# A GRU's recurrent products in two streams, one for each half of the batch

## The chip, the cores and the metric

The kernel runs on one core of a Trainium2 chip. The metric is the device time of one execution in microseconds; a time given as measured is the median of several runs.

## The reference

A GRU runs over 128 time steps for a batch of 64 with 512 features; the hidden size is 512. All is float32.

```
z = sigmoid([x_t, h] @ Wz + bz)
r = sigmoid([x_t, h] @ Wr + br)
h_cand = tanh([x_t, r * h] @ Wh + bh)
h_new = (1 - z) * h + z * h_cand
h_next = tanh(h_new @ Wp + bp)   where (t + 1) % 4 == 0 and t < 127, else h_new
out[t] = x_t + h_new
```

The step takes h_next to the next step. The parts with x_t do not depend on h and can be computed ahead; the parts with h can't.

## The kernel before

Two kinds of matmul share TensorE. The first are the recurrent gates R, Z and H (and P after every fourth step, the tanh above). A gate is `gate` (line 211): for each of four slices k of the hidden size, `products` (line 199) issues four matmuls, for two halves of the batch (h = 0, 1; 32 rows each) and two halves c of the columns. Each writes 32 PSUM partitions, a quarter, so the four stand side by side in the array; half 0 has the first 64 partitions and half 1 the last 64. One such group of four matmuls is called a unit here; a gate is four units of 256 columns. In the profile a float32 matmul is two instructions, so a unit is eight.

The second kind computes the x parts for later steps, by a scheme of products over blocks that needs fewer multiplications (`batch`, line 438), with sums prepared on GpSimd (POOL) and put together there. These are units of 192 columns, 14 to a batch. They stand in a list, and `fill(n)` (line 377) issues the next n of them. They write five scratch PSUM banks, q, r, a, x and y. At the end of certain units ScalarE (ACT) copies a bank to the tiles cx or cq and VectorE (DVE) adds banks into mb; a later unit that writes the bank again waits for that.

A step t issues on PE: gate R; gate Z; fill(places[0]); gate H; fill(places[1]); and if the step has one, gate P; fill(places[2]). The numbers are in PLACES (line 574), by the step's place in a period of eight (u), with HEAD and TAIL for the first and last steps. The order on every engine is the order in which the program issues the instructions; no scheduler changes it.

Behind gate R, for one half after the other, ACT takes the sigmoid (`crossed`, line 226, two instructions), DVE multiplies it with h (rh, line 672) and transposes the product (rhT, line 233): gate H needs it. Behind Z, ACT takes four sigmoids and DVE computes keep = (z - 1) * h (line 686). Behind H, for each half ACT takes the tanh (c), DVE multiplies it with z (line 716) and subtracts keep (line 725); then one transpose of both halves makes hT, which the next gate needs. `seed` (line 368) copies the x parts of the next step into a gate's PSUM tile on ACT as soon as the gate's old content has been read; the matmuls accumulate onto it.

PSUM tiles: rec_r holds R and P, rec_z holds Z and the z values, rec_h holds H and the r values (lines 152 to 160). Each is a bank; accesses of different engines to one bank wait for each other, also to different parts of it.

At the end of a step POOL does sums of the batches and adds h to the x tile, and SyncE (SP) issues the stores and the loads of later x.

Of the kernel before, what the change touches and what calls it, by code (L numbers as in the profile page):

```python
# [18 lines left out]
def kernel(  # L19
# [14 lines left out]
    nc = tc.nc  # L34
# [119 lines left out]
    rec = [ps_c.tile([P, S, 2, J], F32, name=f"rec_{n}") for n in "rzh"]  # L154
    P_ = 3
    r, z = rec[H_][:, 1], rec[Z][:, 1]

    def gate_ps(i):
        return rec[0][:, 1] if i == P_ else rec[i][:, 0]
# [4 lines left out]
    )  # L164

# [33 lines left out]
    def products(ps, lhs, rhs, start=False):  # L199
        for h in range(S):  # L200
            for c in range(2):
                nc.tensor.matmul(  # L202
                    ps[part(2 * h + c)],
                    lhsT=lhs(h),
                    rhs=rhs(c),
                    start=start,
                    stop=True,
                    skip_group_check=True,
                )

    def gate(i, lT, w):
        for k in range(K):
            products(
                gate_ps(i), lambda h: lT[:, h, ts(k, V)], lambda c: quarters(w)[:, c, k]
            )

    def product(ps, lT, w, k, start=False):
        c0, s0 = divmod(k, C)
        products(
            ps.rearrange("p (d j) -> p d j", d=2),  # L220
            lambda h: lT[:, c0, s0 * B + h * V : s0 * B + (h + 1) * V],
            lambda c: quarters(w)[:, c, k],
            start,
        )

    def crossed(dst, h, ps, func):
        for d in range(2):
            nc.scalar.activation(  # L228
                dst[ts(d, 2 * V), h, :], ps[ts(h, 2 * V), d, :], func
            )  # L230
# [137 lines left out]
    def seed(i, t):  # L368
        if t < T:
            nc.scalar.copy(  # L370
                gate_ps(i).rearrange("p d (c n) -> p d c n", c=C),
                G[t][:, :, :, i, :].rearrange("p c d n -> p d c n"),
            )

    queue = []

    def fill(n):
        for _ in range(min(n, len(queue))):
            unit, end = queue.pop(0)
            unit()  # L380
            if end is not None:
                end()
# [13 lines left out]

    def plain(t):
        g, i = divmod(t, Q4)
        order = [(e, k) for e in range(3) for k in range(K)]
        if t == Q4 - 1:  # L400
            order = [(e, k) for k in range(K) for e in range(3)]
        units = [
            lambda e=e, k=k: product(
                banks(t)[e], xT[g][:, i], wx[:, :, e, :], k, k == 0 and e != Z
            )
            for e, k in order
        ]
        return [(u, None) for u in units[:-1]] + [(units[-1], lambda: add_bias(t, (R, Z, H_)))]

    def plain_last():  # L410
        def units(t, gates, ks):
            return [
                lambda e=e, k=k: product(
                    banks(t)[e], xT[LAST][:, t % Q4], wx[:, :, e, :], k, k == 3 and e != Z
                )
                for k in ks
                for e in gates
            ]

        seq = [(u, None) for t in (T - 2, T - 1) for u in units(t, (R, Z, H_), (3,))]  # L420
        for t, gates in ((T - 2, (R, Z, H_)), (T - 1, (R, Z)), (T - 1, (H_,))):
            us = units(t, gates, (2, 0, 1))
            seq += [(u, None) for u in us[:-1]]
            seq.append((us[-1], lambda t=t, gates=gates: add_bias(t, gates)))
        return seq
# [12 lines left out]
    def batch(n, ms):  # L438
# [3 lines left out]
        def unit(ps, m, j, e, start):  # L442
            g, i = ms[m]
            a, b = terms(i)[e]
            left, right = lhs(g, a, j), factor(b, j)
            products(
                ps[:, m].rearrange("p d (g u) -> p d g u", g=3),
                lambda h: left[:, ts(h, V)],
                lambda c: right[:, c::2],
                start and m == 0 and e == 0,  # L450
            )

        def units(ps, j, start):
            return [
                lambda m=m, e=e: unit(ps, m, j, e, start)
# [15 lines left out]
        x_ps = x_two[len(T2) % 2]  # L471
# [26 lines left out]
        for ps, j, start, end in (  # L498
            (a_ps, 2, True, None),
            (x_ps, 7, True, end_x),  # L500
            (q_ps, 1, True, end_q),
            (r_ps, 5, True, end_r),
            (x_ps, 4, False, None),
            (q_ps, 6, False, end_q2),
            (r_ps, 3, False, end_r2),
        ):
            us = units(ps, j, start)
            seq += [(u, None) for u in us[:-1]] + [(us[-1], end)]
# [60 lines left out]
    def pair_right(a, p1, x_, g=1):  # L569
# [5 lines left out]
        (1, 8, 5), (1, 9, 0), (4, 8, 0), (6, 8, 0), (1, 8, 5), (6, 8, 0), (0, 8, 0), (1, 11, 0),  # L575
    )
    HEAD = {0: (12, 12, 0), 1: (8, 6, 0), 2: (16, 12, 0), 3: (8, 6, 8), 4: (6, 10, 0)}
# [10 lines left out]
    h = h_init  # L588
    hT = new_T("hT", "hT_init")
    both = [plain(0), plain(1)]  # L590
    for e in range(3):
        parts = [us[4 * e : 4 * e + 4] for us in both]

        queue.extend(sum(map(list, zip(*parts)), []) if e == R else sum(parts, []))
        fill(4)
        if e == H_:
            for i in range(3):
                seed(i, 0)
        fill(4)
        if e == R:  # L600
            spread(scratch[3], slice(0, 2), (R, H_))
            spread(scratch[1], slice(2, 3), (Z,))
            nc.gpsimd.tensor_sub(bias_d, bias_x[:, 1], bias0)
        if e == Z:
            for s_ in range(S):
                turn(hT[:, s_, :], h[:, s_, :])
# [3 lines left out]
    for t in range(T):  # L610
        g, j = divmod(t, Q4)
        prop = j == CHUNK - 1 and t < T - 1
        last = t == T - 1
        duo, u = divmod(t - 3, 8)
        even, odd = FIRST + 2 * duo, FIRST + 2 * duo + 1
        here = duo >= 0 and even * Q4 < T
        places = HEAD.get(t) or TAIL.get(t) or PLACES[u]
        if t == 0:
            queue.extend(plain(2) + plain(3))
        elif t == 1:  # L620
            queue.extend(batch((1, 0), [(1, 1), (1, 2)]))
        elif t == 2:
            queue.extend(batch((1, 1), [(1, 10), (1, 11)]) + batch((1, 2), [(1, 8), (1, 9)]))
        elif t == 3:
            queue.extend(batches(FIRST))
        elif u == 7:
            queue.extend(batches(even + 2))
        if t == T - 10:
            queue.extend(
# [5 lines left out]
        def join(n):  # L635
            if t == 0:
                join_x(0, 2 + n)
            elif t == 1:
                join_x(1, 2 + n)
            elif t == 2:  # L640
                join_x(2, n)
            elif t == 4:
                join_x(3, 2 * n)
                join_x(3, 2 * n + 1)
            elif duo >= 0 and u in (5, 6):
                join_x(even + 2, 2 * (u - 5) + n)
            elif duo >= 1 and u in (1, 3):
                join_x(odd, u - 1 + n)

        gate(R, hT, wh[R])  # L650
# [17 lines left out]
        rh = two.tile([P, S, J], F32, tag="rh", name=f"rh_{t}")  # L668
        rhT = new_T("rhT", f"rhT_{t}")
        for s_ in range(S):  # L670
            crossed(r, s_, gate_ps(R), AF.Sigmoid)
            nc.vector.tensor_mul(rh[:, s_, :], r[:, s_, :], h[:, s_, :])  # L672
            turn(rhT[:, s_, :], rh[:, s_, :])
        if t != 3:
            seed(R, t + 1)
        if prop:
            nc.scalar.copy(gate_ps(P_), bias_p)
        if last:
            seed(H_, t)
        join(0)  # L680

        gate(Z, hT, wh[Z])
        keep = two.tile([P, S, J], F32, tag="keep", name=f"keep_{t}")
        for s_ in range(S):
            crossed(z, s_, gate_ps(Z), AF.Sigmoid)
        nc.vector.scalar_tensor_tensor(  # L686
            out=keep, in0=z, scalar=1.0, in1=h, op0=ALU.subtract, op1=ALU.mult
        )
        join(1)
        if t == 1:  # L690
            sum_raw34(1)
        if t == 3:
            seed(R, t + 1)
        seed(Z, t + 1)
        if last:
            nc.gpsimd.tensor_sub(xr[g][:, j], xr[g][:, j], keep)
        if t == 0:
            sum_outer()
            for i in (6,):
                sum_inner(i, nc.gpsimd)  # L700
                sum_inner_1(i, nc.gpsimd)
        if t == 2:
            for n in range(2, 4):
                join_x(2, n)
        fill(places[0])
        if t == T - 7:
            reload()

        gate(H_, rhT, wh[H_])
        h_new = two.tile([P, S, J], F32, tag="h", name=f"h_{t}")  # L710
        hT = None if last else new_T("hT", f"hT_{t}")
        cand = two.tile([P, S, J], F32, tag="c", name=f"c_{t}")
        for s_ in range(S):
# [141 lines left out]
```

## Time and profile before

| | |
|---|---|
| measured, median of 3 runs | 1372.75 us (1371.66 to 1373.72) |
| profiled execution, its own time | 1372.32 us |
| its span | 1370.3 us |
| granted TensorE clock, mean over the span | 0.996 |
| busy share: PE, PEld, DVE, ACT, POOL | 96%, 68%, 55%, 53%, 65% |
| first Z gate starts at | 33.48 us |
| last Z gate starts at | 1359.68 us |

A line of the timeline reads: start in us, duration in us, engine, source line, operation, written tile <- read tiles, shape, xcount of merged instructions, and in brackets the engine's idle time before it and what ended it. PE is the matmul, PEld the weight load that goes with each. The ends of matmuls are modelled; their starts are measured.

### The profile page before, as it was taken

Reading aid. Unit: us, or ns where it says so; the run is one execution under the profiler, and the core shown is the slowest. Engines: PE = TensorE matmul, PEld = TensorE weight load, DVE = VectorE, ACT = ScalarE, POOL = GpSimd, SP = SyncE. Lnnn points to the kernel's source line nnn. Section 1 sums busy time; section 2 is a strip of 40 time slices with the busy share of each in tenths; the row PEclk is TensorE's granted clock in tenths of the full one; section 3 lists DMA queues with packets and bytes.
Section 4 is the critical chain, followed back from the end, with each engine's and each line's share of the span. In section 5 each row is a group of like instructions: output and inputs, shape, how many; then the busy total and the mean of one; then the engine's idle time right before and its main releaser. Section 6 shows DMA issues by size and latency. Waiting matters only on the chain. (4 is left out here: it accounts for less than half of the span.)

```text
span 1370.3 us, 60091 instructions
## 1 busy us (share of the span) xinstructions
PE 1315.0 (96%) x26024; PEld 925.3 (68%) x26024; DVE 753.5 (55%) x2036; ACT 730.2 (53%) x2401; POOL 887.3 (65%) x1030
## 2 busy tenths in 40 slices
PE   7999999999999999999999999999999999999986
PEld 3566767676676766767676676766767676676654
DVE  1645555555555555556555555555556555555533
ACT  1345555555555555555555555555555555555544
POOL 3577757777576766757777576776757767576420
PEclk9999999999999999999999999999999999999999
DMA  8401112101111111112101111111111101111030
GB/s 188 99 19 49 48 41 57 34 20 47 49 49 34 36 50 30 49 38 54 39 19 48 49 49 34 36 46 34 49 36 52 44 19 49 49 33 34 17 102 17
DMA packets 114705, 63.15 MB, mean 46 GB/s; under 512 B 13160, under 2 KB 109672, under 8 KB 114440
## 3 DMA queue, kind: packets, MB, share of 16 engines
q1 hardware_dynamic: 113412, 58.44, 17.0%
q8 instruction: 204, 3.34, 1.1%
q10 hardware_dynamic: 772, 0.72, 0.2%
q14 instruction: 61, 0.50, 0.1%
q0 software_dynamic: 256, 0.14, 0.1%
HBM read 42.47 MB, written 16.78 MB: 43 GB/s over the span
## 5 line engine op out<-in xcount | busy, mean ns | idle before, releaser
L228 ACT ACTIVATE rec_h<-rec_r 64x128 f32<-64x128 f32 x512 | 128.0, 250 | 344.2 <-PE rec_r L202 288.3
L202 PE MATMUL rec_h<-wh,rhT 128*32 128x256 f32 x4096 | 274.2, 381 | 4.3 <-DVE rh L672 3.7
L202 PEld LDWEIGHTS rec_h<-wh,rhT 128*32 128x32 f32 x4096 | 166.4, 110 | 75.0 <-DVE rh L672 24.7
L202 PE MATMUL rec_r<-wh,hT 128*32 128x256 f32 x3072 | 184.9, 381 | 14.4 <-DVE hT L233 13.3
L202 PE MATMUL rec_z<-wh,hT 128*32 128x256 f32 x3072 | 183.8, 379 | 0.0
L792 POOL TENSOR_TENSOR xr<-xr,h 128x256 f32<-128x256 f32 x127 | 93.1, 733 | 134.4 <-DVE h L725 123.0
L228 ACT ACTIVATE c<-rec_h 64x128 f32<-64x128 f32 x512 | 139.3, 272 | 68.0 <-PE rec_h L202 61.6
L526 POOL TENSOR_TENSOR cp<-mb,mb 128x768 f32<-128x768 f32 x75 | 137.1, 1828 | 43.5 <-DVE mb L495 39.9
L526 POOL TENSOR_TENSOR mb<-mb,mb 128x768 f32<-128x768 f32 x58 | 106.2, 1830 | 82.7 <-DVE mb L495 82.7
L202 PEld LDWEIGHTS rec_r<-wh,hT 128*32 128x32 f32 x3072 | 96.6, 110 | 87.2 <-DVE hT L233 27.2
L672 DVE TENSOR_TENSOR rh<-rec_h,h 128x128 f32<-128x128 f32 x192 | 55.9, 291 | 172.6 <-ACT rec_h L228 172.6
L202 PEld LDWEIGHTS rec_z<-wh,hT 128*32 128x32 f32 x3072 | 103.8, 110 | 61.9
L228 ACT ACTIVATE rec_z<-rec_z 64x128 f32<-64x128 f32 x512 | 128.0, 250 | 22.3 <-PE rec_z L202 7.2
L716 DVE TENSOR_TENSOR rec_z<-c,rec_z 128x128 f32<-128x128 f32 x256 | 75.7, 296 | 99.2 <-ACT c L228 82.5
L526 POOL TENSOR_TENSOR cp<-mb 128x768 f32<-128x768 f32 x47 | 86.2, 1835 | 60.7 <-DVE rec_z L716 59.2
L468 ACT COPY cq<-scratch_q 128x384 f32<-128x384 f32 (+1 forms) x214 | 102.3, 478 | 21.8 <-PE scratch_q L202 19.5
L531 POOL TENSOR_TENSOR mb<-mb,bias_x 128x768 f32<-128x768 f32 x35 | 64.2, 1833 | 45.5 <-DVE mb L495 45.5
L686 DVE SCALAR_TENSOR_TENSOR keep<-rec_z,h 128x256 f32<-128x256 f32 x96 | 40.8, 425 | 91.4 <-ACT rec_z L228 91.4
L491 DVE TENSOR_TENSOR mb<-scratch_q,cx 128x384 f32<-128x384 f32 (+1 forms) x107 | 58.1, 543 | 49.0 <-ACT cq L468 49.0
L233 DVE STREAM_TRANSPOSE rhT<-rh 128x128 f32<-128x128 f32 x256 | 79.8, 312 | 8.7
L725 DVE TENSOR_TENSOR h<-rec_z,keep 128x128 f32<-128x128 f32 x254 | 74.0, 292 | 16.4
L370 ACT COPY rec_z<-cp 128x256 f32<-128x256 f32 x128 | 48.2, 377 | 61.9 <-DVE keep L686 61.9
(157 smaller groups left out, 2805.6 us busy)
## 6 DMA issues: line engine op xcount, KB each, us to landing
out_dram<-xr SPq DMA_DIRECT2D x249, 64.0 KB, 1.8
xr<-in_x_dram SPq DMA_DIRECT2D x248, 64.0 KB, 2.2
xs<-in_x_dram SPq DMA_DIRECT2D x240, 64.0 KB, 2.2
wx<-in_L_cond_Wz_dram SPq DMA_DIRECT2D x4, 256.0 KB, 8.4
wx<-in_L_cond_Wh_dram SPq DMA_DIRECT2D x4, 256.0 KB, 10.3
wh<-in_L_cond_Wr_dram SPq DMA_DIRECT2D x4, 256.0 KB, 9.0
wh<-in_L_cond_Wz_dram SPq DMA_DIRECT2D x4, 256.0 KB, 4.4
wh<-in_L_cond_Wh_dram SPq DMA_DIRECT2D x4, 256.0 KB, 8.0
```

Source lines behind the costliest of these rows:

```text
L202: nc.tensor.matmul(ps[part(2 * h + c)], lhsT=lhs(h), rhs=rhs(c), start=start, stop=True, skip_group_check=True,)
L228: nc.scalar.activation(dst[ts(d, 2 * V), h, :], ps[ts(h, 2 * V), d, :], func)
L233: nc.vector.transpose(out=dst, in_=src)
L370: nc.scalar.copy(gate_ps(i).rearrange("p d (c n) -> p d c n", c=C), G[t][:, :, :, i, :].rearrange("p c d n -> p d c n"),)
L468: nc.scalar.copy(c[:, :nm], ps[:, :nm])
L491: nc.vector.tensor_add(blocks(1, 1), runs(q_ps[:, :nm]), runs(T2[what][:, :nm]))
L526: nc.gpsimd.tensor_add(dst, a, b)
L531: nc.gpsimd.tensor_add(m, m, v.unsqueeze(1).to_broadcast([P, 2, 3 * J]))
L672: nc.vector.tensor_mul(rh[:, s_, :], r[:, s_, :], h[:, s_, :])
L716: nc.vector.tensor_mul(c, cand[:, s_, :], c)
L725: nc.vector.tensor_sub(h_new[:, s_, :], c, keep[:, s_, :])
L792: nc.gpsimd.tensor_add(xr[g][:, j], xr[g][:, j], h_new)
```

## The change

The two halves of the batch become two streams. A Python generator `half(h)` issues the whole sequence of all steps for one half: its products of a gate or a fill unit are now two matmuls. After every unit a stream hands back its columns, and a loop merges the two streams by columns issued: half 1 starts 700 columns behind, and whichever stream has issued fewer goes next. So on PE's queue half 0's units alternate with those of an earlier part of half 1's sequence.

- PSUM by halves: bank rec_0 holds R and H (or P) of half 0, rec_1 those of half 1, rec_z as before. The r values of both halves share one place, the free end of the scratch bank r.
- R, H and P seeds are copied by halves (64 rows each); the Z seed stays one copy, behind half 1's Z and keep.
- The transposes of h are by halves. The four sigmoids of Z and keep stay together, behind half 1's Z.
- A fill unit is issued twice, once for each half; its copies and additions follow half 1's. Where a unit writes a bank that is read after an earlier unit, half 0 waits in the order until half 1 has issued that earlier unit.
- PLACES and one entry of HEAD are different; the sum over eight steps is 98 units in both. In the fifth step of a period sum_s34(odd) goes ahead of outer_c21(even).
- The work on POOL and SP that stood behind the step stands behind half 1's step.

The diff, cut (`...` marks what is left out):

```diff
-    rec = [ps_c.tile([P, S, 2, J], F32, name=f"rec_{n}") for n in "rzh"]
+    rec = [ps_c.tile([P, 2, 2, J], F32, name=f"rec_{n}") for n in ("0", "1", "z")]
+    z = rec[2][:, 1]
+    def gate_ps(i, h):
+        return rec[2][:, 0] if i == Z else rec[h][:, 0 if i == R else 1]
+    r_ = scratch[r_bank][:, 3 * J :]
...
+    def products(ps, h, left, rhs, start=False):
+        for c in range(2):
+            nc.tensor.matmul(
+                ps[part(2 * h + c)], lhsT=left, rhs=rhs(c), start=start, stop=True,
+                skip_group_check=True,
+            )
+    def gate(i, h, lT, w):
+        for k in range(K):
+            products(gate_ps(i, h), h, lT[:, h, ts(k, V)], lambda c: quarters(w)[:, c, k])
+            yield S * J
...
+    def seed(i, t, h):
         if t < T:
+            rows = slice(None) if i == Z else ts(h, 2 * V)
             nc.scalar.copy(
+                gate_ps(i, h)[rows].rearrange("p d (c n) -> p d c n", c=C),
+                G[t][rows, :, :, i, :].rearrange("p c d n -> p d c n"),
             )
...
+    def put(units):
+        for unit, cols, bank, end, read in units:
+            queue.append((unit, cols, reader.get(bank, -1), end))
+            for b in read:
+                reader[b] = len(queue) - 1
+    def fill(n, h):
+        for _ in range(n):
+            if place[h] == len(queue):
+                return
+            unit, cols, after, end = queue[place[h]]
+            while h == 0 and after >= place[1]:
+                yield 0
+            unit(h)
+            yield cols
+            place[h] += 1
+            if h == 1 and end is not None:
+                end()
...
     PLACES = (
-        (1, 8, 5), (1, 9, 0), (4, 8, 0), (6, 8, 0), (1, 8, 5), (6, 8, 0), (0, 8, 0), (1, 11, 0),
+        (0, 8, 6), (0, 8, 0), (6, 8, 0), (6, 8, 0), (0, 8, 6), (0, 8, 0), (6, 8, 0), (6, 6, 0),
     )
-    HEAD = {0: (12, 12, 0), 1: (8, 6, 0), 2: (16, 12, 0), 3: (8, 6, 8), 4: (6, 10, 0)}
+    HEAD = {0: (12, 12, 0), 1: (8, 6, 0), 2: (16, 12, 0), 3: (8, 6, 8), 4: (6, 8, 0)}
...
+                elif u == 4:
+                    if odd < LAST:
+                        sum_s34(odd)
                     outer_c21(even)
                     if odd < LAST:
                         outer_1(odd)
-                        sum_s34(odd)
...
+    def half(h):
+        for t in range(T):
...
+            yield from gate(R, h, hT, wh[R])
...
+            crossed(r_, h, R, AF.Sigmoid)
+            nc.vector.tensor_mul(rh[:, h, :], r_, h_old[:, h, :])
+            turn(rhT[:, h, :], rh[:, h, :])
+            if t != 3:
+                seed(R, t + 1, h)
...
+            yield from gate(Z, h, hT, wh[Z])
+            if h == 1:
+                for i in range(S):
+                    crossed(z[:, i, :], i, Z, AF.Sigmoid)
+                nc.vector.scalar_tensor_tensor(
+                    out=keep, in0=z, scalar=1.0, in1=h_old, op0=ALU.subtract, op1=ALU.mult
+                )
...
+                seed(Z, t + 1, 0)
...
+            yield from fill(places[0], h)
...
+            yield from gate(H_, h, rhT, wh[H_])
+            crossed(cand[:, h, :], h, H_, AF.Tanh)
+            c = z[:, h, :]
+            nc.vector.tensor_mul(c, cand[:, h, :], c)
...
+            nc.vector.tensor_sub(h_new[:, h, :], c, keep[:, h, :])
+            turn(hT[:, h, :], h_new[:, h, :])
+            if prop:
+                nc.scalar.copy(gate_ps(P_, h)[ts(h, 2 * V)], bias_p[ts(h, 2 * V)])
+            elif t < T - 2:
+                seed(H_, t + 1, h)
+            state[t + 1] = h_new, hT
+            yield from fill(places[1], h)
...
+            if prop:
+                yield from gate(P_, h, hT, wp)
...
+                yield from fill(places[2], h)
+            if h == 1:
+                behind_step(t, duo, u, h_new)
+
+    LAG = 700
+    halves = [half(0), half(1)]
+    at = [0, LAG]
+    live = [True, True]
+    while any(live):
+        h = 0 if live[0] and (not live[1] or at[0] <= at[1]) else 1
+        cost = next(halves[h], None)
+        if cost is None:
+            live[h] = False
+        elif cost == 0:
+            at[0] = at[1] + 1
+        at[h] += cost or 0
```

## The prediction

> **What bounds the kernel now.** I read the page first: engines, then the granted clock.
>
> ```profile
> span 1370.3 us, 60091 instructions
> PE 1315.0 (96%) x26024; PEld 925.3 (68%) x26024; DVE 753.5 (55%) x2036; ACT 730.2 (53%) x2401; POOL 887.3 (65%) x1030
> PEclk9999999999999999999999999999999999999999
> ```
>
> TensorE is the engine, at full clock. But the 96% is made of modelled ends and hides short waits, so I work from starts, in the timeline of PE:
>
> ```profile
> 700.04 0.51 PE L202 MATMUL scratch_r<-tw,s4r 128*32 128x192 f32 x8
> 700.36 0.51 PE L202 MATMUL scratch_r<-wx,s12r 128*32 128x192 f32 x8
> ...
> 702.62 1.91 PE L202 MATMUL rec_z<-wh,hT 128*32 128x256 f32 x32
> 704.35 0.51 PE L202 MATMUL scratch_y<-tt,xT 128*32 128x192 f32 x8
> ```
>
> Eight 192-column instructions (one fill unit) start every 0.325 us (over longer runs; 0.32 here). A gate, 32 instructions of 256 columns in four units, takes 1.726 us when nothing waits (702.62 to 704.35), 0.4315 a unit. Now the period. Steps repeat by eights; call them u0 to u7, u0 and u4 being those with the P gate. The Z gates of one period start at 661.68, 673.86, 682.88, 692.68, 702.62, 714.92, 725.03, 733.81 and 744.05. The period is 82.37 us (the windows, with the busy time inside it):
>
> ```profile
> 661.68:744.05 82.37, 80.75 (x1621) 57.57 (x1617) 47.05 (x127) 46.05 (x151) 56.69 (x67) 1.00 0.16 41
> ```
>
> The columns are PE, PEld, DVE, ACT, POOL busy, clock, DMA share. PE's work in a period is 26 gates x 1.726 = 44.9 and 98 fill units x 0.325 = 31.8, together 76.7. So 5.6 us of each 82.4 are waits. By step, u0 to u7, measured minus work: 0.73, 0.59, 0.72, 0.21, 0.85, 0.38, 1.00, 1.16. What they wait for is seen in u6 (timeline of all engines; the last column is what ended an idle time):
>
> ```profile
> 725.03 1.91 PE L202 MATMUL rec_z<-wh,hT 128*32 128x256 f32 x32
> 725.34 0.53 ACT L228 ACTIVATE rec_h<-rec_r 64x128 f32<-64x128 f32 x2 [2.17 <-PE rec_r L202]
> 725.90 0.29 DVE L672 TENSOR_TENSOR rh<-rec_h,h 128x128 f32<-128x128 f32 x1 [1.47 <-ACT rec_h L228]
> ...
> 727.14 0.14 PEld L202 LDWEIGHTS rec_h<-wh,rhT 128*32 128x32 f32 x4 [0.68 <-DVE rh L672]
> ...
> 727.25 1.09 ACT L228 ACTIVATE rec_z<-rec_z 64x128 f32<-64x128 f32 x4
> ...
> 728.84 0.38 ACT L370 COPY rec_z<-cp 128x256 f32<-128x256 f32 x1 [0.49 <-DVE keep L686]
> 728.89 0.33 PE L202 MATMUL scratch_y<-tt,o 128*32 128x192 f32 x2
> ...
> 729.02 0.39 PE L202 MATMUL rec_h<-wh,rhT 128*32 128x256 f32 x2
> 729.05 0.68 PE L202 MATMUL scratch_y<-tt,o 128*32 128x192 f32 x10
> ...
> 729.46 1.13 ACT L228 ACTIVATE c<-rec_h 64x128 f32<-64x128 f32 x4 [0.24 <-PE rec_h L202]
> ...
> 732.08 1.93 PE L202 MATMUL rec_r<-wh,hT 128*32 128x256 f32 x32
> ```
>
> Gate H could start at 725.03 + 1.73 = 726.76, but waits to 727.14 for half 1's rh, which reads r in H's bank. R could start 8 units after H, and waits for the transpose of both halves' h (731.49 to 731.94). POOL (57 of 82 us) and DMA (16%) hold nothing up. The chain that ended last holds only the closing microsecond.
>
> **The change part by part.**
>
> *Latency of one half.* From this timeline (rh's transpose runs 726.23 to 726.54; the second c is multiplied at 730.84, subtracted from at 731.17), counted from a gate's end on PE: R: 0.31 to ACT, 0.56 to rh, 0.33 to the transpose, 0.31 for it, 0.06 to PE: 1.57. H: 0.31, two tanh 0.58, then 0.33, 0.32, 0.31, 0.06: 1.91. Before, R waits for both halves' H chain: 729.46 - 0.31 to 732.05 is 2.90. After, each half waits for its own: 1.57 against gate Z (1.73) as cover, and 1.91 against 8 fill units (2.60) or, in u7, 6 (1.95). P's chain, 0.31 + 0.58 + 0.31 + 0.06 = 1.26, lies under 6 units. The wait for the other half's rh goes too: r_ moves to scratch_r's bank, which PE next writes in a fill.
>
> *What is late next.* After half 1's Z gate ACT does four sigmoids, waits for keep, and copies the Z seed: 1.59 from first sigmoid to the seed (727.25 to 728.84) and 0.38, so 1.97. In ACT's order half 0's tanh stands behind this. The steps u0, u1, u4, u5 have no fill between Z and H. Count from half 0's R end. Lag: 700 x 1.726 / 1024 = 1.18. Half 1's Z ends at 1.18 + 1.73 = 2.91; ACT is free at 2.91 + 0.31 + 1.97 = 5.19; half 0's H ended at 3.45 and asked for ACT at 3.76. Its transposed h is there at 5.19 + 1.91 - 0.31 = 6.79, and its next gate is due at 3.45 + 2.60 = 6.05: a wait of 0.74, and half 1's products behind it on PE's queue stop with it. Half 1 meanwhile finishes the unit it is in, so the lag shrinks by up to a unit: counting units, about 124 columns, 0.21. That gives 0.53. I take 0.57, nearer the second, because the lag is set by the previous such wait: 4 x 0.57 = 2.3.
>
> *The other four steps.* Six fill units between Z and H put half 0's tanh at 3.45 + 1.95 + 0.31 = 5.71, after 5.19. In u2 and u3 a cq copy (0.48) follows the Z seed and three adds on DVE follow it (0.46 apart): 5.19 + 0.48 + 3 x 0.46 = 7.05, where half 0's product wanted DVE at 5.71 + 0.58 = 6.29. It is 0.76 late with a slack of 2.60 - 1.91 = 0.69: 0.1 each. In u6 and u7 the first unit after H writes the x bank, whose copy waits behind the Z seed: done at 5.19 + 0.48 = 5.67, wanted at 3.45 + 1.95 = 5.40: 0.3, or 0.1 with the shorter lag; u7 has 0.1 more, its cover being 6 units. Together 0.6. Restarting after a wait costs some 0.02 (a first start-to-start of 0.24 for 0.216), 0.2 in all. Sum 3.1 a period against 5.6.
>
> *Copies by halves.* R, H and P seeds become two 64-row copies: 18 more a period. Cost by the row of the 128-row copy (0.38), since length along a partition is the same: 6.8 us, ACT 46 to 53 of about 80 (bounds 0.25, the 64x128 sigmoid, and 0.38). Covered: the R seed ends 0.31 + 0.56 + 0.38 = 1.25 after R, before H at 1.73. hT's transpose by halves: 2 x 0.31 for 0.45. POOL's and SP's work keeps its order except sum_s34(odd), which goes ahead of c21 in u4; that puts 3.4 us before c21, whose result the steps two later need. SP's DMA issues do not change in number and stand behind half 1's step: cover is a step.
>
> *Two widths side by side.* Not run as such before, but the rows at 728.89 to 729.05 show it in small: half 1's last 256-wide pass beside half 0's 192-wide ones, 0.13 out of step after the wait at 727.14, each at its own pace. I take 0; bounds: 0 by this row, and 0.25 of the lag (1.18 x 64/256 = 0.3) at each of 28 borders between gate and fill if a half's next pass waited for the other's: 8.3 a period. A gain below 0 is excluded, each pass has its length.
> The Trainium skill, "TensorE: Matmul & The Clock Gate", section "Packing small matmuls — row/col tiling", says that matmuls start and end strictly in program order. By it the sum would be about 1450. Here half 0's scratch_y starts at 728.89 before half 1's last rec_h at 729.02, which comes before it in the program, so the row decides.
>
> *Head and tail.* In the last six steps (cover of 3 to 5 units) the wait after H is about 2.6 now (9.09 - 3 x 1.726 - 3 x 0.325 = 2.9 in one) and 2.1 to 2.3 after: 3 us. Head (44.6 us for three steps): 0.
>
> *Sum.* Steps 4 to 118 are 14.3 periods: 14.3 x (5.6 - 3.1) = 36, and 3: 39 off 1372.3, the profiled execution's own time (span 1370.3 and 2.0 around it; 0.4 below the median): 1333.
>
> **The rivals.** (1) *Nearly all goes*: the lag settles a full unit shorter (444 columns, 0.75), the short-step wait is 0.31 and the period 78.3: 14.3 x 4.0 + 3 off, 1312. For it: waits reset the lag. Against: program order only lets it shrink to a unit's boundary. (2) *The wait moves and eats the gain*: ACT, 66% busy, makes half 1 late too; a short-step wait of 1.1 and 0.2 more in the others gives about 5.4 a period: 1366. Against: half 1's tanh can start at 5.19 + 0.58 + 0.38 = 6.15, its h is there at 7.75, and its gate, put off with half 0's, is due at 4.63 + 2.60 + 0.74 = 7.97. (3) *Slower: the halves fall in step at their borders*: 8.3 a period more, 14.3 x (8.3 - 2.5) - 3 = +80, about 1450; it decides from 0.09 a border (2.5 / 28), and half the bound gives 14.3 x 1.65 - 3, 1393. For it: runs of one width beside the other are 1.2 us long there, 0.2 us here. (4) *It does not do it*: PE has one queue, and if each half's waits stop the other at other times, they add up to what both share now: 1370. Against: in my count only half 0 waits.
>
> **How the numbers follow.** Mine 0.55 (1318 to 1352 by waits of 0.3 and 0.9 in short steps), (1) 0.19, (2) 0.08, (3) 0.14, (4) 0.04. The range runs from (1), 1302 with restarts and the other steps at nothing too (0.2 + 0.5 a period), to 1372; outside lie (3) and a little of (1) and (2). A measurement tells 0.2%, 2.7 us, from nothing. Faster is mine, (1) and three quarters of (2), 0.80; same (4) and a little of (2), 0.05; slower (3) and the rest, 0.15.
>
> **What would show it.** A period of about 80 us; ACT busy 53 in it; PE's wait for rh gone; waits of 0.5 to 0.7 on half 0's hT in u0, u1, u4, u5, with the Z seed just ahead of c on ACT; gate passes at 0.216 beside fill passes at 0.162. Wrong if the passes of one width are stretched beside the other, or if POOL or a scratch bank's copy releases PE in most steps.

## The result and the profile after

The changed kernel takes 1340.73 us (median of 4 runs, 1340.09 to 1342.19) against 1372.7 us of the kernel before on the same chip (4 runs, 1371.66 to 1373.72): a ratio of 0.977, interval 0.975 to 0.979. Forecast were 1333, range 1302 to 1372. The profiled run took 1340.09 us.

The page of the changed kernel (engines, granted clock, and one row of the costliest groups, which gives busy time, mean ns of one, and the idle time before it):

```profile
span 1338.2 us, 60949 instructions
PE 1283.7 (96%) x26024; PEld 1117.0 (83%) x26024; DVE 771.2 (58%) x2163; ACT 837.1 (63%) x2688; POOL 886.3 (66%) x1030
PEclk8989999999999999999999999999999999999999
...
L371 ACT COPY rec<-cp 64x256 f32<-64x256 f32 x512 | 189.9, 371 | 33.4 <-DVE cp L409 9.6
```

TensorE has the same 26024 matmuls and 31 us less modelled busy time; its share is still 96%, so the share again says little. The 512 copies of 64 rows take 371 ns each, the copies of 128 rows before took 377: half the rows save next to nothing. The clock, all nines before, is at 8 in two of the first three slices; the second of these is taken up under head and tail.

One period, from Z gate to Z gate (windows; PE, PEld, DVE, ACT, POOL busy, clock, DMA share):

```profile
646.21:725.99 79.78, 78.33 (x1622) 70.14 (x1618) 48.16 (x137) 52.75 (x169) 56.60 (x67) 1.00 0.16 42
```

The work on PE is 76.7 as before, so 3.06 us are waits (before 5.6). By step, u0 to u7: 0.76, 0.69, 0.04, 0.04, 0.64, 0.64, 0.11, 0.14. What is left lies in the short steps. The timeline of u1, all engines:

```profile
661.49 1.09 ACT L230 ACTIVATE rec_z<-rec_z 64x128 f32<-64x128 f32 x4 [0.58 <-PE rec_z L204]
...
662.62 0.42 DVE L821 SCALAR_TENSOR_TENSOR keep<-rec_z,hprop 128x256 f32<-128x256 f32 x1 [0.94 <-ACT rec_z L230]
...
663.08 0.38 ACT L371 COPY rec_z<-cp 128x256 f32<-128x256 f32 x1 [0.49 <-DVE keep L821]
...
663.47 0.55 ACT L230 ACTIVATE c<-rec 64x128 f32<-64x128 f32 x2
...
664.70 0.31 DVE L233 STREAM_TRANSPOSE hT<-h 128x128 f32<-128x128 f32 x1
...
665.16 0.41 PE L204 MATMUL rec<-wh,hT 128*32 128x256 f32 x2 [0.27 <-DVE hT L233]
```

Read the column of starts: four sigmoids of Z at 661.49, the Z seed 1.59 later (it sat 0.49 for keep), and half 0's tanh directly behind it at 663.47, with no idle time noted before it: ACT's order, not PE, sets when it starts. From there 1.69 us to half 0's next gate on PE, which waits for hT. The waits over the whole span (us, times, longest) say the same:

```profile
ACT rec_z L371 <- DVE keep L821: 61.8, 126, 0.5
...
PE rec L204 <- DVE hT L233: 26.7, 60, 1.6
...
PE rec L204 <- ACT rec L371: 7.7, 5, 4.4
```

PE's wait for rh, which held up 75 gates H before, has no row under that name any more. What is left of it stands under ACT. The row of the kernel before, then that of the changed kernel (waits):

```profile
PEld rec_h L202 <- DVE rh L672: 24.7, 75, 0.7
```

```profile
PEld rec L204 <- ACT scratch_r L230: 9.7, 27, 0.6
```

All 27 are gates H of u0 and u1. The third row of the list above is small in number but long (4.4 us), and is taken up under the head.

Where the 32 us come from, by starts of Z gates in the two profiled executions: from step 4 to step 118 the kernel before took 1173.46 us and the changed one 1136.83, so 36.6 less. Up to step 4 it is 2.6 us later (98.39 against 95.82), and from step 118 to the end 2.0 us longer (103.0 against 101.0). 36.6 - 2.6 - 2.0 = 32.0, the difference of the spans (1370.3 and 1338.2).

### The profile page after: what moved, and what is told of

Same layout as the page of the kernel before. It is cut to its first block, busy times and chain, and to the rows that moved or that the text cites. A ratio compares the mean times of both kernels' runs of the same rounds, so it can differ in the third digit from the quotient of the medians.

```text
span 1338.2 us, 60949 instructions
## 1 busy us (share of the span) xinstructions
PE 1283.7 (96%) x26024; PEld 1117.0 (83%) x26024; DVE 771.2 (58%) x2163; ACT 837.1 (63%) x2688; POOL 886.3 (66%) x1030
## 4 chain that ended last, share of the span: by engine, by line
PE 77%; ACT 9%; DVE 7%; DMA 3%; issue 2%; POOL 1%; SPq 1%; DVEq 0%; ACTq 0%; POOLq 0%
PE rec L204 35%; PE rec_z L204 15%; PE scratch_r L204 10%; PE scratch_q L204 9%; ACT rec_z L230 5%; PE scratch_x L204 3%; PE scratch_y L204 3%; PE scratch_a L204 3%; ACT c L230 2%; DVE keep L821 2%; ACT rec_z L371 2%; DVE hT L233 1%; DVE rec_z L849 1%; DVE h L858 1%; DMA wx<-in_L_cond_Wr_dram 1%
## 5 line engine op out<-in xcount | busy, mean ns | idle before, releaser
L204 PE MATMUL rec<-wh,rhT 128*32 128x256 f32 x4096 | 375.2, 381 | 4.6 <-ACT rec L371 4.4
L204 PE MATMUL rec<-wh,hT 128*32 128x256 f32 x3072 | 277.9, 380 | 14.7 <-DVE hT L233 14.7
L204 PEld LDWEIGHTS rec<-wh,rhT 128*32 128x32 f32 x4096 | 232.4, 110 | 35.6 <-ACT scratch_r L230 9.7
L230 ACT ACTIVATE scratch_r<-rec 64x128 f32<-64x128 f32 x512 | 128.0, 250 | 166.6 <-PE rec L204 95.6
L371 ACT COPY rec<-cp 64x256 f32<-64x256 f32 x512 | 189.9, 371 | 33.4 <-DVE cp L409 9.6
L204 PEld LDWEIGHTS rec<-wh,hT 128*32 128x32 f32 x3072 | 165.5, 110 | 48.0 <-ACT c L230 27.9
L230 ACT ACTIVATE c<-rec 64x128 f32<-64x128 f32 x512 | 139.0, 272 | 26.1 <-PE rec L204 16.8
L204 PE MATMUL scratch_r<-wx,s12r 128*32 128x192 f32 x1056 | 120.9, 327 | 0.0
L204 PE MATMUL scratch_r<-tw,s 128*32 128x192 f32 x928 | 117.2, 326 | 0.0
L204 PE MATMUL scratch_r<-wx,s 128*32 128x192 f32 x928 | 107.3, 326 | 0.0
L849 DVE TENSOR_TENSOR rec_z<-c,rec_z 128x128 f32<-128x128 f32 x256 | 73.7, 288 | 54.8 <-ACT c L230 53.9
```

Of the source, the lines that this page charges most:

```text
L204: nc.tensor.matmul(ps[part(2 * h + c)], lhsT=left, rhs=rhs(c), start=start, stop=True, skip_group_check=True,)
L230: nc.scalar.activation(dst[ts(d, 2 * V)], gate_ps(i, h)[ts(h, 2 * V), d, :], func)
L371: nc.scalar.copy(gate_ps(i, h)[rows].rearrange("p d (c n) -> p d c n", c=C), G[t][rows, :, :, i, :].rearrange("p c d n -> p d c n"),)
L849: nc.vector.tensor_mul(c, cand[:, h, :], c)
```

## Experiments

All start from the changed kernel (1340.7 us). A kernel that was run once has one time, and the first three steps of the kernel, which wait for the first loads, scatter: in the runs of the table the Z gate of step 3 started anywhere between 76.6 and 79.7 us, and at 81.9 with the lag of 900. So differences of 3 us and less are read from the trace and not from the time. The kernel before took 1373.1 to 1374.9 us (medians) beside them. The parts of each profiled execution, in us, from the starts of Z gates:

| kernel | step 3 (Z gate of 3 to 4) | step 4 to step 118 | step 118 to the end |
|---|---|---|---|
| before | 17.7 | 1173.5 | 101.0 |
| changed | 21.2 | 1136.8 | 103.0 |
| e2, seed behind half 0's tanh | 21.2 | 1112.8 | 100.6 |
| e9, seed behind half 1's tanh | 21.6 | 1103.2 | 95.6 |
| e4, lag 500 | 20.2 | 1127.2 | 99.9 |
| e5, lag 900 | 21.3 | 1195.2 | 108.8 |
| e6, lag 0 | 20.3 | 1133.2 | 98.2 |
| e7, R seeds of step 3 later | 19.3 | 1137.0 | 103.0 |
| e8, fill units of T - 6 later | 21.6 | 1137.1 | 100.6 |
| e11, e9 + e7 + e8 | 15.9 | 1103.5 | 95.4 |
| e12, e11 with lag 500 | 16.1 | 1103.8 | 93.2 |

### Half 0's tanh behind the Z seed

The theory: in the short steps half 0 waits because its tanh stands on ACT behind the Z seed, which waits for keep. Two runs move the seed from its place behind keep, once behind half 0's tanh and once behind half 1's:

```diff
 e2_seed_late
-                seed(Z, t + 1, 0)
...
             crossed(cand[:, h, :], h, H_, AF.Tanh)
+            if h == 0:
+                seed(Z, t + 1, 0)
 e9_seed_last
-                seed(Z, t + 1, 0)
...
+            if h == 1:
+                seed(Z, t + 1, 0)
             state[t + 1] = h_new, hT
             yield from fill(places[1], h)
```

> The Z seed is copied behind half 0's tanh instead of ahead of it; z stays in its PSUM bank. Theory A: half 0's tanh starts when the four sigmoids are done, about 0.8 earlier, but the product with z then waits for the seed in z's bank, so 0.1 to 0.3 of wait is left in the four short steps: 1308 to 1318. Theory B: at most the copy's own 0.38 us in four steps, 22 us less, 1319, with half 1's tanh later by the same 0.38 and so likely nothing: 1319 to 1341.

> The Z seed is copied behind half 1's tanh, subtraction and H seed, so neither half's product with z waits for it; z stays in PSUM. Theory A: half 0's tanh starts at 4.1 after its R's end, its h is there at 5.7, due at 6.05: no wait in the short steps, a period near 77.2 and 1304 (1300 to 1312), some 10 below the run with the seed between the two. Theory B: no better than that run, 1316.

Measured: 1316.11 and 1301.36 us; periods of 78.05 and 77.41. The waits of e2 by step are 0.31, 0.24, 0, 0, 0.19, 0.19, 0, 0.38, those of e9 0.46, 0.22 and six times 0. The timeline of e9, u1:

```profile
647.35 1.09 ACT L230 ACTIVATE rec_z<-rec_z 64x128 f32<-64x128 f32 x4 [0.58 <-PE rec_z L204]
...
648.47 0.55 ACT L230 ACTIVATE c<-rec 64x128 f32<-64x128 f32 x2
...
650.68 0.38 ACT L371 COPY rec_z<-cp 128x256 f32<-128x256 f32 x1 [0.28 <-DVE h L857]
```

The tanh now starts 1.12 after the first sigmoid instead of 1.98, and the waits of the short steps u4 and u5 are gone. The theory holds: ACT's order was the price: 33.6 us of the 39 in the steady part, and 7.4 in the last steps, which have little or no fill between Z and H either (the first steps of this run were 2 us later). Of the 7.4, 3.5 lie in steps T - 6 and T - 5, where another wait, for a load, got shorter too (see head and tail). The 0.46 and 0.22 that are left in u0 and u1 are waits of gate H: it starts 2.18 and 1.94 us after gate Z there (medians of ten periods), 1.73 in u4 and u5. The sigmoid of R is late in these two steps, because r shares scratch_r's bank with a fill's result (see the lag of 900 below).

### The same wait, taken away in another manner

The seed waits for keep because z lies in the bank that the seed writes. Putting z into SBUF takes that wait away and leaves the order of the instructions alone; e3 adds the edit of e2.

```diff
 e1_z_sbuf (e3_both: this and e2)
-    z = rec[2][:, 1]
             keep = new_two("keep", t)
+            z = new_two("z", t)
```

> Theory A (the waits of 0.64 to 0.76 us in u0, u1, u4, u5 come from ACT's order: the Z seed, held by keep because z lies in its bank, stands ahead of half 0's tanh): with the z values in SBUF the seed no longer waits for keep, 0.49 us less on that path in each of four steps, so waits of about 0.2 there, a period near 77.9 instead of 79.78, and 14.3 x 1.9 = 27 us less: 1313 (1306 to 1322). Theory B (those waits are a half's own latency with ACT 66% busy, wherever the seed stands): no change, 1341, or some us more because DVE and ACT now use SBUF for z.

> z in SBUF and the Z seed behind half 0's tanh. Theory A: no wait is left in the short steps, the period goes to 77.2 us: 14.3 x 2.6 = 37 us less, 1304 (1300 to 1310), below each alone. Theory B: as each alone, 1319 or more.

Measured: 1480.83 and 1475.78 us, 140 us slower; neither theory. What DVE does with z became slow. The instructions of one line (count, then shortest, median and longest ns), first of e1, then of the changed kernel:

```profile
L858 DVE TENSOR_TENSOR h<-z,keep x254: 291/363/1847, 47.2 to 1467.0; 128x128 f32<-128x128 f32 x127
```

```profile
L858 DVE TENSOR_TENSOR h<-rec_z,keep x254: 290/291/292, 46.2 to 1326.3; 128x128 f32<-128x128 f32 x127
```

The shortest is the same. The long ones stand beside POOL's adds (timeline of e1):

```profile
655.35 1.82 POOL L555 TENSOR_TENSOR mb<-mb,mb 128x768 f32<-128x768 f32 x1 [3.62 <-DVE mb L523]
655.57 1.75 DVE L858 TENSOR_TENSOR h<-z,keep 128x128 f32<-128x128 f32 x1
...
657.13 1.87 POOL L560 TENSOR_TENSOR mb<-mb,bias_d 128x768 f32<-128x768 f32 x1
...
657.59 1.56 DVE L849 TENSOR_TENSOR z<-c,z 128x128 f32<-128x128 f32 x1
657.81 0.41 PE L203 MATMUL rec<-wh,hT 128*32 128x256 f32 x2 [0.85 <-DVE hT L232]
```

Of e1's instructions on the three lines that read z and a second SBUF operand, those with POOL idle take 0.29 (L849, L858) and 0.43 (keep), as ever; beside a POOL operation they take up to 1.72, 1.85 and 2.12. So these two runs say nothing on keep's wait. They say that z in PSUM is worth more than the wait it costs. The Trainium skill, "SBUF — State Buffer", section "Who interferes with whom", has the rule: a VectorE instruction with two SBUF inputs takes its second through a read interface that it shares with GpSimd, and contends there with a GpSimd instruction that reads SBUF; the section calls the sharing an exclusive lock. The rows above agree with it.

### The lag

```diff
-    LAG = 700
+    LAG = 500      (e4_lag500; 900 in e5_lag900, 0 in e6_lag0)
```

> Half 1 stands 500 columns behind instead of 700. Theory A: half 1's Z gate, and with it the sigmoids and the seed, ends 200 columns = 0.34 us sooner after half 0's H gate began; the short waits go from 0.68 to about 0.35: 14.3 x 4 x 0.34 = 19 us less, 1322 (1318 to 1332). Theory B: the two halves' chains come closer together on ACT, so the same or more: 1341 to 1355.

> Half 1 stands 900 columns behind. Theory A (half 1's Z sigmoids and the Z seed stand ahead of half 0's tanh on ACT): they come 200 columns = 0.34 us later, the short waits go from 0.68 to about 1.0: 14.3 x 4 x 0.34 = 19 us more, 1360 (1350 to 1366). Theory B (the waits are a half's own latency): the halves are further apart on ACT, so the same or less, 1335 to 1341.

> Both halves issue in step, with all else of the change in place. If the lag brings the gain: half 1's sigmoids of R stand behind half 0's and behind half 0's seed, its rh is transposed at 2.5 after R where H is due at 1.73, and its tanh stands behind half 0's: about 1.05 of wait in each short step, 0.3 in the long ones, 0.9 in u7, 5.9 a period, 40 us more than with the lag: 1381 (1365 to 1395), no better than the kernel before. If the halves' own banks and seeds bring it: 1341 to 1350.

Measured: 1328.45 with 500, 1408.97 with 900 and 1332.39 with none. A longer lag costs, as the theory of ACT's order says, but its sizes are off. With 500 the four short waits are 0.56 each, and not 0.35. At 900 the loss is more than three times the forecast: the waits are 1.62, 1.55, 0.37, 0.37, 1.19, 1.19, 0.43, 0.46. There a second thing is added (timeline of e5, u1):

```profile
692.51 0.53 ACT L230 ACTIVATE scratch_r<-rec 64x128 f32<-64x128 f32 x2 [1.15 <-DVE mb L523]
...
693.86 0.41 PE L204 MATMUL rec<-wh,rhT 128*32 128x256 f32 x2 [0.43 <-ACT scratch_r L230]
```

r now lies in scratch_r's bank; its sigmoid waits until DVE has read the fill's result out of that bank (L523), and half 1's late fill makes that late: in u0 and u1 R's sigmoid starts 1.03 us after gate Z does, with a lag of 700 it is 0.60, and 0.23 in the steps without this wait.

That no lag at all does better than 700 (by 3.7 us in the steady part and 4.8 in the last steps) is against the theory that the lag brings the gain (1381), and some 9 us below the least that the other theory said. On ACT the halves part by themselves (timeline of e6):

```profile
657.67 0.53 ACT L230 ACTIVATE scratch_r<-rec 64x128 f32<-64x128 f32 x2 [1.24 <-PE rec L204]
...
658.24 0.37 ACT L371 COPY rec<-cp 64x256 f32<-64x256 f32 x1
...
658.63 0.54 ACT L230 ACTIVATE scratch_r<-rec 64x128 f32<-64x128 f32 x2
```

On ACT half 1's R crossing stands behind half 0's crossing and seed, 0.96 later; so do the tanh, 0.98 apart (661.77 and 662.75). With lags of 500 and 700 the distance on ACT is the same, 0.95 to 1.04; with 900 it is up to 1.36 in four of the eight steps. On PE the lag does set the distance. From the start of half 0's gate Z to the sigmoids behind half 1's it is 2.35 us with no lag, 2.78 with 500, 2.95 to 3.07 with 700 and 3.28 to 3.94 with 900 (medians of ten periods for each step). So a shorter lag brings half 0's tanh forward, but half 1's stays 0.98 behind it. In e6, u1, half 0's hT is there at 663.32 and its gate starts unhindered at 663.91; PE then stops from 664.14 to 664.46 for half 1's hT, which ends at 664.31. The wait has changed halves. Of the four lags 500 is the best, 6.0 us better than none in the steady part.

### The banks by half

```diff
 e10_gate_banks
-    rec = [... for n in ("0", "1", "z")]
-        return rec[2][:, 0] if i == Z else rec[h][:, 0 if i == R else 1]
+    rec = [... for n in "rzh"]
+        return rec[0][:, 1] if i == P_ else rec[i][:, 0]
```

> The changed kernel with one part undone: the PSUM banks are again by gate (rec_r, rec_z, rec_h, as before), the streams, the lag of 700, the seeds by halves and r_ in scratch_r's bank are kept. Theory A (it is the bank of its own that lets a half go on while the other's result is read; the lag alone gives nothing): when half 0's R, H or P gate ends, half 1 is about two units into the same gate in the same bank; its other units wait for half 0's crossing, 0.31 + 0.58 = 0.9 us, and half 0's products behind them with them. 18 such gates a period x 0.9 = 16 us, less at most the 3.1 us of waits there are now: period 92 to 96, time 1341 + 14.3 x (13 to 16) = 1527 to 1570. Theory B (splitting the waits by halves is enough, the banks do not matter): 1341, or 1337 since R's and H's seeds no longer share a bank in step 3.

Measured: 1689.77 us, a period of 102.41, so 25.7 of waits. The side of theory A, and more of it. The timeline (R gate):

```profile
629.66 0.53 ACT L230 ACTIVATE scratch_r<-rec_r 64x128 f32<-64x128 f32 x2 [1.03 <-PE rec_r L204]
...
630.27 0.37 ACT L371 COPY rec_r<-cp 64x256 f32<-64x256 f32 x1
...
630.70 0.41 PE L204 MATMUL rec_r<-wh,hT 128*32 128x256 f32 x2 [0.96 <-ACT rec_r L371]
630.71 0.11 PEld L204 LDWEIGHTS rec_z<-wh,hT 128*32 128x32 f32 x2
630.71 0.41 PE L204 MATMUL rec_z<-wh,hT 128*32 128x256 f32 x2
```

Half 1's other products of gate R wait not only for half 0's crossing but for the seed behind it, which is written into the same bank: 0.31 + 0.53 + 0.08 + 0.37 + 0.06 = 1.35 in place of the 0.9 that I had counted. Times 18 gates that is 24.3 (an estimate from this one gate), near the 25.7. Half 0's next products (rec_z) start with half 1's and not before. So two streams on banks by gate are 23% slower than the kernel before: the gain hangs on the halves having no bank in common at R, H and P. The Trainium skill, "PSUM — Partial Sum Buffer", section "PSUM bank collisions raise a hardware error", says that accesses to different quadrants of 32 partitions in one bank do not collide; half 0 reads partitions 0 to 63 while half 1 writes 64 to 127. By it this wait comes from dependencies kept by whole banks and not from the memory; no run here shows the case without the wait. Nor does a run undo the new PLACES or the seeds by halves alone, so their shares in the gain are not shown.

### Head and tail

In step 3 the R seed takes a cp that POOL makes late. The lines of the kernel before, then of the changed kernel (timelines):

```profile
82.41 1.91 PE L202 MATMUL rec_h<-wh,rhT 128*32 128x256 f32 x32
85.64 0.38 ACT L370 COPY rec_r<-cp 128x256 f32<-128x256 f32 x1 [4.30 <-POOL cp L526]
```

```profile
85.77 0.76 ACT L371 COPY rec<-cp 64x256 f32<-64x256 f32 x2 [4.46 <-POOL cp L556]
...
86.19 0.64 PE L204 MATMUL rec<-wh,rhT 128*32 128x256 f32 x2 [4.39 <-ACT rec L371]
```

The seed comes at the same time in both. Before, gate H ran ahead of it, in a bank of its own; now R and H of a half share a bank, and H waits 4.39. e7 puts these seeds behind the tanh:

```diff
 e7_head
-                if t == 3:
-                    for i in range(S):
-                        seed(R, t + 1, i)
             crossed(cand[:, h, :], h, H_, AF.Tanh)
+            if t == 3:
+                seed(R, t + 1, h)
```

> In step 3 alone the late R seed (its x part comes from POOL) is issued behind the tanh instead of ahead of gate H. If the 3.5 us that this step lost come from R and H now sharing a bank (H's products wait for R's seed), step 3 goes from 21.2 to about 17.7 us and the time to 1337. If they come from POOL's work itself, which R of step 4 needs anyway, the wait moves to the next gate: 1341.

Measured: 1338.22 us, 2.5 less, and the period that begins with step 3 takes 88.09 in place of 90.03. Gate H no longer waits, so the shared bank was the cause. But only 1.9 of the 3.5 us of step 3 come back. The timeline of e7 shows what is late next:

```profile
85.74 0.38 ACT L371 COPY rec_z<-cp 128x256 f32<-128x256 f32 x1 [4.49 <-POOL cp L556]
...
86.67 0.36 PE L204 MATMUL scratch_x<-tt,xT 128*32 128x192 f32 x2 [3.10 <-ACT cx L497]
```

The Z seed waits for the same cp, and behind it on ACT stand the copy of a fill's bank, for which PE stops, and the tanh (86.88). The kernel before has this order too. What it does not have is a slower clock. The same stretch in the kernel before, then in the changed kernel (windows; PE, PEld, DVE, ACT, POOL busy, clock, DMA share):

```profile
84.30:91.20 6.90, 3.64 (x80) 2.40 (x80) 3.92 (x10) 3.37 (x10) 1.38 (x2) 1.00 0.01 2
```

```profile
84.30:91.20 6.90, 5.00 (x56) 3.92 (x60) 1.61 (x4) 2.88 (x8) 1.44 (x1) 0.51 0.00 0
```

Around the stop of 4.39 us the granted clock was one half, and the gate's products behind it started at half the pace. By an estimate from the 5.00 us that PE was busy, this costs 2.5 us, as much as the head lost in all (2.6). In e7 the clock is 0.50 from 87.4 to 90.8, behind the stop of 3.10; that is 1.7 us by the same estimate. In the kernel before PE stops 2.56 us there, and the clock stays at 1.00. No run holds the clock fixed, so the shares of stop and clock are not taken apart by experiment. In the table's column of step 3, the runs with 20.2 and 20.3 have about 3.4 us of the half clock there, those with 21.2 to 21.6 about 6.8.

In the tail, PE waits for the second load of wx (timeline of the changed kernel, step T - 6):

```profile
1283.67 0.41 PE L204 MATMUL scratch_q<-wx,xT 128*32 128x256 f32 x2 [1.61 <-DMA wx<-in_L_cond_Wz_dram]
...
1286.38 0.64 PE L204 MATMUL scratch_r<-wx,xT 128*32 128x256 f32 x2 [2.08 <-DMA wx<-in_L_cond_Wh_dram]
```

```diff
 e8_tail
-        T - 6: (0, 4, 0), T - 5: (0, 3, 0),
+        T - 6: (0, 1, 0), T - 5: (0, 6, 0),
```

> The changed kernel with three fill units moved from step T - 6 to step T - 5, so that the fill that reads the reloaded wx starts a step later. Theory A (step T - 6's 3.7 us, 1.61 + 2.08, are waits for that reload, which lands too late now that the steps before it are shorter): 1337 to 1338. Theory B (the wait moves with the fill, or step T - 6 then waits for its own hT, having less cover): 1340 to 1342.

Measured: 1340.11 us. The waits for the load are gone, and in their place stand (timeline of e8):

```profile
1287.04 0.41 PE L204 MATMUL rec<-wh,hT 128*32 128x256 f32 x2 [2.51 <-DVE hT L233]
...
1289.44 0.84 PE L204 MATMUL rec<-wh,hT 128*32 128x256 f32 x10 [0.91 <-DVE hT L233]
```

With one fill unit behind H, hT is late. Steps T - 6 and T - 5 together take 22.06 in place of 24.62: 2.6 gained of 3.7, in this one run hidden by a head that was 2.2 us longer (step 4's Z gate at 100.58). The trace shows theory A for the cause of the old waits and theory B for what comes next: the new waits are 3.42 us against 3.69. Part of what is gained all the same is the clock. In the changed kernel it falls behind these waits (windows), in e8 it is 1.00 throughout these steps:

```profile
1285.80:1289.20 3.40, 2.81 (x28) 1.58 (x32) 0.12 (x1) 0.00 (x0) 0.57 (x1) 0.50 0.24 67
```

That is 1.4 us by the estimate above. Why the load lands too late is seen beside the kernel before (SP's issues; before, then changed):

```profile
1305.72 1.74 SPq L97 DMA_DIRECT2D wx<-in_L_cond_Wr_dram  x4
```

```profile
1272.73 1.75 SPq L97 DMA_DIRECT2D wx<-in_L_cond_Wr_dram  x4
```

Before, the reload went out 3.60 us after the Z gate of step T - 7 (at 1302.12), now 4.80 after it (at 1267.93): in the program it stands behind half 1's fill units. And the loads of Wh took 7.5 us from issue to landing where they took 5.3, those of Wz 6.5 and 5.7 (medians); why, is not shown. Step T - 7 itself is not shorter, 10.06 against 9.94 us, so the expectation's reason (shorter steps) does not hold.

### All together

e11 joins e9, e7 and e8; e12 is e11 with a lag of 500.

> Three edits together, all tried or under trial alone: the Z seed behind half 1's tanh, step 3's R seeds behind the tanh, three fill units from T - 6 to T - 5. They lie in different steps, so they add: 1301.4 - 2.5 - 3 = 1296 (1293 to 1300); 1299 if the tail's edit brings nothing. Ratio to the kernel before 0.944.

> The same with a lag of 500 in place of 700. In the changed kernel that was worth 12 us, because half 0's tanh, fixed by ACT's order behind the Z seed, then met a later half 0. With the Z seed last, half 0's tanh waits for nothing of half 1's but its Z sigmoids, done some 1.1 us after half 1's Z; waits are left in u0 and u1 only (0.7 us a period), and these may go: 14.3 x 0.7 = 10 at most, 1286 to 1297. If the waits of u0 and u1 are not of the lag: 1296 as with 700.

Measured: e11 1295.10 us (4 runs, 1293.34 to 1295.62), a ratio to the kernel before of 0.9431, interval 0.9415 to 0.9447; e12 1292.43 us (1291.49 to 1293.53), 0.9416, interval 0.9402 to 0.9430. e11 comes within 1 us of the sum, but the parts are other ones: step 3 gives 5.6 us against e9, since neither seed stands ahead of the tanh any more and the clock stays at 1.00 there, where e7 alone gave 1.9; and the tail's edit gives 0.3 where it alone gave 2.4. The lag, worth 9.6 us in the steady part before, gives nothing there now: with half 0's tanh free of the seed, the period does not depend on it. The medians of e12 and e11 are 2.7 us apart; of the 4.0 between the two profiled executions 2.1 lie in the head, which scatters, and 2.1 in the last steps. e12's page and one of its rows of costliest groups:

```profile
span 1289.7 us, 60849 instructions
PE 1266.8 (98%) x26024; PEld 1033.0 (80%) x26024; DVE 775.6 (60%) x2163; ACT 834.7 (65%) x2688; POOL 886.7 (69%) x1030
...
L204 PE MATMUL rec<-wh,hT 128*32 128x256 f32 x3072 | 265.6, 379 | 2.2 <-DVE hT L233 2.2
```

The wait for hT fell from 26.7 us over the span to 2.2. A period is 0.75 above PE's own 76.7. e12 is 48 us faster than the changed kernel and 81 faster than the kernel before.

## Why the prediction was right, and where it was off

- **Latency of one half.** Right in the main. The wait for the other half's rh is gone, and so is the wait for its chain of H. From tanh to the next gate it is 1.69 where I had 1.60.
- **What is late next.** Right in place, cause and size: the waits are in u0, u1, u4 and u5, with the Z seed just ahead of the tanh on ACT, 1.59 and 0.38 as counted; 0.64 to 0.76 each where I took 0.57. e2 and e9 show the cause. The 0.1 more in u0 and u1 goes with r's new bank, which my sentence on r_ looked at only for PE's writes: DVE reads that bank as well, R's sigmoid starts 0.37 later there, and gate H 1.94 after gate Z in place of 1.73. In e9, where ACT's order no longer counts, these waits of gate H are the only ones left.
- **The lag in this count.** The distance was right, what depends on it was not. I took 0.97 (1.18 less 0.21); on PE half 1's gate Z ends 0.93 us behind half 0's (2.97 less the 1.73 and 0.31 of my count). Rival (1) has a distance of 0.75 and waits of 0.31. The lag of 500 gives nearly that distance (2.78 less 2.04, 0.74), but waits of 0.56: my sum looks at half 0 alone, and there PE stops a second time, for half 1's hT (e4, u1: 661.97 to 662.28), whose tanh stands 0.98 behind half 0's on ACT.
- **The other four steps.** 0.04, 0.04, 0.11 and 0.14, together 0.33, where I had 0.1, 0.1, 0.1 to 0.3 and 0.1 more, together 0.6, and 0.2 for restarts. In all 3.06 against 3.1, and 36.6 us against 36 for the steady part. So close an agreement is luck: the short steps were 0.43 above the 2.3 of the sum, the other terms 0.47 below.
- **Copies by halves.** Right: 371 ns for 64 rows, ACT 52.75 busy in a period where I had 53.
- **Two widths side by side.** Right with 0. The PE timeline of the changed kernel, at a border between gate and fill:

```profile
675.14 0.41 PE L204 MATMUL rec<-wh,hT 128*32 128x256 f32 x2
675.29 0.33 PE L204 MATMUL scratch_r<-tw,s 128*32 128x192 f32 x2
675.36 0.41 PE L204 MATMUL rec<-wh,hT 128*32 128x256 f32 x2
675.45 0.33 PE L204 MATMUL scratch_r<-tw,s 128*32 128x192 f32 x2
675.57 0.41 PE L204 MATMUL rec<-wh,hT 128*32 128x256 f32 x2
```

  256 columns start every 0.215, and 192 columns between them every 0.16, each at its own pace in these rows. Rival (3) is out. The rule of strict program order that the prediction weighed, by which the time would have been about 1450, does not hold between the two halves in these rows.
- **Head and tail: the step that failed.** I took 0 for the head and -3 for the tail; it was +2.6 and +2.0, 7.6 us in all, nearly the whole distance from 1333 to 1340.7. For the head I looked at the banks by half only in the eight steps of a period, where no seed is late. In step 3 one is, by 4.4 us, and the bank that R and H now share hands that on to gate H: step 3 takes 21.20 where it took 17.73 (it also began 0.9 earlier, while the seed came at the same time). For the tail I counted only shorter hT waits. These came (without the load's wait the last steps are some 1.7 us shorter, without the half clock behind it too some 3.1), but the reload of wx goes out 1.2 us later in its step and takes longer, and step T - 6 waits 3.7 us for it. In both places the sum had full clock throughout; the half clock behind these stops makes about 2.5 and 1.4 us of the 7.6, by the estimates above.
- **The other rivals.** (2), the wait moves and eats the gain, was right that a wait moves, but it leaves 3.06 a period and not the 5.4 that the rival asked for. (4), that the waits of both halves add up, falls with 3.06 of waits against 5.6.
- The words of the change put the lag first. The runs say that it is the least of it: two streams pay only with banks of their own for the halves (1340.7 against 1689.8 without them), and the lag of 700 costs 8 to 12 us against 0 or 500.

## What to carry to other kernels

When one stream is split into two that cover each other's waits, list for each in-order engine between them what now stands ahead of the earlier half's work: one copy that waits for the later half (0.4 us of work, 0.5 of waiting) took more here than the whole change brought: to issue it later gave 39 us. Then go through every bank that has new tenants, in the first and last steps too, where something is late that is never late in the steady part. And ask of a staggering constant what it sets: here it set the distance on TensorE, while on ACT the halves stood about 1.0 apart with 0, 500 and 700 alike; 500 was the best of the four tried, and once the seed was moved, 500 and 700 gave the same period. Look at the granted clock around every stop of TensorE, too: the products behind it may run slower.

## What the runs showed of the hardware

- An fp32 operation of two tensors on VectorE took 0.29 us with one input in PSUM, whatever POOL did (290 to 292 ns over 254 of them), and with both inputs in SBUF 0.29 beside an idle POOL but up to 1.85 beside POOL's adds of 1.82. This made a kernel 10% slower by a move that should have removed a wait.
- Matmuls of the two halves, 256 columns in one and 192 in the other, start every 0.215 and every 0.16 us side by side; neither takes on the other's pace.
- The granted TensorE clock was 0.50 for 6.9 us around a stop of 4.39 us (step 3 of the changed kernel) and for 3.4 us behind one of 3.10 (e7); behind stops of 2.56 (the kernel before) and 2.51 (e8) it stayed at 1.00.
